# A two-layer graph network on one core: groups of four neighbouring runs of nodes, packed as the mean is transposed

## The chip, the cores and the metric

The kernel runs on one core of one Trainium2 chip. The metric is the device time of one execution in microseconds (us). Before the change the median of three runs is 2605.41 us (2605.15 to 2607.06). The engines are called PE (matmul; PEld its weight load), DVE, ACT, POOL and SP; SP and POOL issue DMAs.

## The reference

The graph has 6250 nodes with rows of 512 floats, and 106250 edges: 50000 random pairs in both directions, and one loop on every node, sorted by `dst`. All is fp32.

```python
# layer 0: mean over the incoming edges, two dense products, residual, layernorm
x_l = x @ W_l.T + b_l
agg = segment_sum(x_l[src], dst);  deg = segment_sum(1, dst)
x = layernorm(x + agg / max(deg, 1) + x @ W_r.T)
# layer 1: mean over the edges by src, relu, residual, layernorm with gamma, beta; then once more
neigh = segment_sum(x[dst] @ W_neigh.T + b_neigh, src) / max(deg, 1)
y = x + relu(x @ W_self.T + b_self + neigh)
x = layernorm(x + layernorm(y) * gamma + beta)
```

The kernel sums the rows of neighbours first and multiplies the mean by the weights afterwards, which is the same by linearity.

## The kernel before, in words

**Tiling.** The sorted edges are cut into chunks of 128, M = 831 in layer 0. Layer 1 needs them by `src`; a sort on the chip, whose steps are spread between the groups of layer 0 (`more(1, True)` and `more(5, False)` in the loop), gives 782 chunks without the loops: every node has one, so layer 1 adds a node's own row instead, and the few loops that occur more than once are found by `loops_beyond_one` and kept apart in `more`.

A **run** is the nodes that begin within 3.5 chunks (`PAIR` = 7 halves; 3 in layer 1, `PAIR_L` = 6), at most H = 32 of them. `place` (L440 on) reads each run's first node from the sorted keys into `lo` (matmul L456) and builds `rel`, the place of each edge's node within its run. If a run had over 32 nodes, or some other condition did not hold, a flag would send the layer to `plain`, a slow loop. There are NW = 238 runs in layer 0, 261 in layer 1. A **group** g is four *distant* runs, c*Q + g for c = 0 to 3, with Q = 60 groups in layer 0 and 66 in layer 1. Run c of the group uses partitions 32c to 32c + 31 in all that follows.

**One group** passes these steps:

- `fetch` (L608): POOL gathers the source rows of each chunk, one indirect DMA of 128 rows for one chunk (L604), into tiles `rows` of four chunks, one of each run. There are `CHUNKS` = 10 buffers; a group takes 3.5 tiles in layer 0 and 3 in layer 1. A tile on the border of two groups is visited by both.
- `match` (L628): one DVE operation compares `rel` with 0 to 31 and gives one-hot matrices `hot`, 128x32 for each chunk and run; `shrink` (L636): ACT copies them to bf16.
- `visits` (L685): PE adds `hot`.T @ rows into `agg` in PSUM, one matmul of 128x32 weights and 512 columns for each chunk and run (L694). The four runs' matmuls lie in four strips of the array side by side; I call the four (eight instructions in fp32) a quad. In layer 1 there is one quad more, with the rows of the repeated loops (`more_rows`).
- `count` (L697): PE sums the one-hots into `deg` (L703); `inverse` (L553): DVE makes `inv` = 1/deg (L557 in layer 1, L560 in layer 0).
- `average` (L708): in layer 1 DVE adds the group's own rows to `agg` (L712); then ACT makes `mean` = agg * inv (L714).
- `turn` and `transposed` (L566): PE transposes `mean` or `own` in four blocks with the identity (L569) into PSUM `tp`, and ACT copies it to SBUF (L571).
- `dense`, `project` (L574): four matmuls of 128x128 weights and 512 columns with each of two weights, into `po` (L577).
- `close`, `finish0`, `finish1`: residual, relu and layernorm on DVE, with ACT for the root (L509).
- `begin` (L669): the group's own rows come in four loads of 32 rows, 64 KB each, on SP (L682); the first row of each is a value in SBUF that SP reads into a register first (L644).
- `store` (L732): four stores of 32 rows from SP, each with such a register (L743). Rows behind a run's last node are overwritten by the run that follows. For three groups (`ends`), POOL stores by indirect DMA instead (L736); in layer 1 these are groups 61, 62 and 65.

**Order.** Instructions run on each engine in the order in which the program names them. The loop (L761 to L790) names for g: fetch and match of g + 1; visits of the first two tiles of g; turn of mean and dense of own of g − 1; store of g − 2; begin of g + 1; visit of the third tile; dense of mean of g − 1; turn of own of g; the other visits, count and average of g; close of g − 1; steps of the sort; shrink of g + 1. So POOL's row of gathers runs ahead as far as there are buffers.

Of the kernel before, what the change touches and what calls it, by code (L numbers as in the profile page):

```python
# [9 lines left out]
F32 = mybir.dt.float32  # L10
# [8 lines left out]
P = 128  # L19
C = 4  # L20
H = P // C
PAIR = 7
PAIR_L = 6
# [75 lines left out]
def kernel(  # L99
# [53 lines left out]
    last, middle = [const.tile([P, P], F32, name=n) for n in ("last", "middle")]  # L153
    for t, row in ((last, P - 1), (middle, P // 2 - 1)):
        nc.vector.tensor_scalar(t, ones, pidx, None, op0=ALU.mult)
        nc.vector.tensor_scalar(t, t, float(row), None, op0=ALU.is_equal)
# [52 lines left out]
    class Sorter:  # L209


        def __init__(self, key, val, layer, pool, ps, loops):
# [4 lines left out]
            pair = self.pair = PAIR_L if loops else PAIR  # L217
            self.half = (pair + 1) // 2
            self.vis = self.half + 1
            self.NW = (2 * self.M + pair - 1) // pair  # L220

            self.Q = (self.NW + 2 * C - 1) // (2 * C) * 2
            Q = self.Q
# [7 lines left out]
            self.X = 1 if loops else 0  # L231
            self.rel = const.tile([P, Q, self.X + self.vis, C], F32, name=f"rel{layer}")
            self.flag = const.tile([1, 1], I32, name=f"flag{layer}")
            if loops:

                a = (E - N - CAP - 1) // P
                self.row = pool.tile([P, M - a], F32, name="row")
                nc.gpsimd.iota(self.row, pattern=[[P, M - a]], base=a * P - (E - N) + LOOP,
                               channel_multiplier=1, allow_small_or_imprecise_dtypes=True)
                self.more = const.tile([P, 1], F32, name="more")  # L240
                self.more_i = const.tile([P, 1], I32, name="more_i")
# [144 lines left out]
        def loops_beyond_one(self):  # L386
# [51 lines left out]
            nc.vector.tensor_scalar(none, self.more, float(N - 1), None, op0=ALU.min)  # L438
            nc.vector.tensor_copy(self.more_i, none)

        def place(self):

            lo, pad, Q, NW = self.lo, self.padded, self.Q, self.NW
            pair, half, vis = self.pair, self.half, self.vis
            mid = middle if pair % 2 else last
            nc.vector.memset(pad[:, 0:1], float(NONE))
            bad = self.fresh()[:1, :2 * NW + C + 2]
            nc.vector.memset(bad, 0.0)
            if self.loops:
                nc.vector.tensor_copy(bad[:, 2 * NW + C:], self.odd)  # L450
            ends = self.ps.tile([P, 2 * D], F32, name="turn")
            ne, no = (NW + 1) // 2, NW // 2

            for a, sel, off, n in ((0, last, 0, ne), (D // 2, mid, half, no),
                                   (D, last, pair - 1, ne - 1), (D + D // 2, last, half - 1, no)):
                nc.tensor.matmul(ends[:, a:a + n], sel, bass.AP(  # L456
                    tensor=pad.tensor, offset=pad.offset + off,
                    ap=[list(pad.ap[0]), [pair, n]]), start=True, stop=True)
            nc.vector.memset(lo, float(N))
            nc.vector.tensor_copy(view(lo, (0, 2, ne, 1)), ends[:, :ne].unsqueeze(2))  # L460
            nc.vector.tensor_copy(view(lo, (1, 2, no, 1)),
                                  ends[:, D // 2:D // 2 + no].unsqueeze(2))
# [4 lines left out]
            nc.vector.tensor_tensor(bad[:, :NW], lo[:1, 1:NW + 1], lo[:1, :NW], op=ALU.subtract)  # L467
            nc.vector.tensor_scalar(bad[:, :NW], bad[:, :NW], float(H), None, op0=ALU.is_gt)
            one = lo[:1, :]
            nc.vector.tensor_tensor(bad[:, NW:NW + ne - 1].unsqueeze(2),  # L470
                                    view(one, (2, 2, ne - 1, 1)),
                                    ends[:1, D:D + ne - 1].unsqueeze(2), op=ALU.is_equal)
            nc.vector.tensor_tensor(bad[:, NW + ne - 1:2 * NW - 1].unsqueeze(2),
                                    view(one, (1, 2, no, 1)),
                                    ends[:1, D + D // 2:D + D // 2 + no].unsqueeze(2),
                                    op=ALU.is_equal)
            for i, (w, e) in enumerate([(Q * c - 2, Q * c) for c in range(1, C)] + [(NW - 3, NW)]):
                t = bad[:, 2 * NW - 1 + i:2 * NW + i]
                nc.vector.tensor_tensor(t, lo[:1, e:e + 1], lo[:1, w:w + 1], op=ALU.subtract)
                nc.vector.tensor_scalar(t, t, float(H), None, op0=ALU.is_lt)  # L480
# [4 lines left out]
            for c in range(C):  # L485
                for i, off in ((0, 0), (1, half)):
                    nodes = bass.AP(tensor=pad.tensor, offset=pad.offset + pair * Q // 2 * c + off,
                                    ap=[list(pad.ap[0]), [pair, Q // 2], [1, vis]])
                    rel = self.rel.rearrange("p (q i) v c -> p q i v c", i=2)[:, :, i, self.X:, c]
                    first = view(lo, (c * Q + i, 2, Q // 2, 1))  # L490
                    nc.vector.tensor_tensor(rel, nodes, first.to_broadcast([P, Q // 2, vis]),
                                            op=ALU.subtract)
            if self.loops:
                nc.vector.tensor_scalar(
                    self.rel[:, :, 0, :], lo[:, :C * Q].rearrange("p (c q) -> p q c", c=C), -1.0,
                    self.more, op0=ALU.mult, op1=ALU.add)
# [56 lines left out]
    def inverse(deg, nr, work, loops=False):  # L553

        inv = work.tile([P, 1], F32, name="inv")
        if loops:
            nc.vector.tensor_scalar(inv[:nr], deg, 1.0, None, op0=ALU.add)  # L557
            nc.vector.reciprocal(inv[:nr], inv[:nr])
            return inv, None
        nc.vector.tensor_scalar(inv[:nr], deg, 1.0, None, op0=ALU.max)  # L560
        nc.vector.reciprocal(inv[:nr], inv[:nr])
        some = work.tile([P, 1], F32, name="some")
        nc.vector.tensor_scalar(some[:nr], deg, 1.0, None, op0=ALU.min)  # L563
        return inv, some

    def transposed(v, nr, name, work, ps):  # L566
        p = ps.tile([P, NK, P], F32, name="tp")
        for k in range(NK):
            nc.tensor.transpose(p[:, k, :nr], v[:nr, k * P:(k + 1) * P], ident[:nr, :nr])  # L569
# [10 lines left out]
    def grouped(s, table, w_n, w_s, layer, finish, dest, other):  # L580


        with tc.tile_pool(name=f"g{layer}", bufs=2) as work, tc.tile_pool(
            name=f"gp{layer}", bufs=1, space=PSUM
        ) as ps:
            M, NW, Q = s.M, s.NW, s.Q
            chunks, hots, state = {}, {}, {}
            ends = Q - 1, (NW - 1) % Q, (NW - 2) % Q
# [6 lines left out]
            def windows(g):  # L595
                return [c for c in range(C) if c * Q + g < NW]

            def own_tiles(g):

                return range(g // 2 * s.pair + (s.half if g % 2 else 0),  # L600
                             g // 2 * s.pair + (s.pair if g % 2 else s.half))

            def gather(t, m):
                nc.gpsimd.indirect_dma_start(  # L604
                    out=t, out_offset=None, in_=table,
                    in_offset=bass.IndirectOffsetOnAxis(ap=s.idx[:, m:m + 1], axis=0))

            def fetch(g):  # L608
                if g == 0 and s.loops:
                    rows = work.tile([P, D], F32, name="more_rows", bufs=1)  # L610
                    nc.gpsimd.indirect_dma_start(
                        out=rows, out_offset=None, in_=table,
                        in_offset=bass.IndirectOffsetOnAxis(ap=s.more_i[:, :1], axis=0))
                    chunks["more"] = {c: rows for c in range(C)}
                for t in ([-1] if g == 0 else []) + list(own_tiles(g)):
                    rows = work.tile([P, C, D], F32, name="rows", bufs=CHUNKS)
                    chunks[t] = {}
                    for c in windows(g):
                        m = c * (Q // 2 * s.pair) + t
                        if 0 <= m < M:  # L620
                            gather(rows[:, c, :], m)
                            chunks[t][c] = rows[:, c, :]

            def visit_tiles(g):
                t = own_tiles(g)
                return ["more"] * s.X + list(range(t.start - 1, t.stop))

            def match(g):  # L628
                hot = work.tile([P, (s.X + s.vis) * C, H], F32, name="hot")
                n = len(visit_tiles(g)) * C  # L630
                both(hot[:, :n], s.rel[:, g].rearrange("p v c -> p (v c)")[:, :n].unsqueeze(2)
                     .to_broadcast([P, n, H]),
                     cols.unsqueeze(1).to_broadcast([P, n, H]), ALU.is_equal)
                hots[g] = hot

            def shrink(g):  # L636
                hb = work.tile([P, (s.X + s.vis) * C, H], BF16, name="hotb", bufs=1)
                n = len(visit_tiles(g)) * C
                nc.scalar.copy(hb[:, :n], hots[g][:, :n])  # L639
                hots[g] = (hots[g], hb)  # L640

            def start(w, t):

                return nc.values_load(  # L644
                    s.lo_i[:1, w:w + 1], engines=[ENG.SP], min_val=0, max_val=t.shape[0] - H,
                    skip_runtime_bounds_check_because="the windows hold: N - H at most, or N "
# [294 lines left out]
```

## Time and profile before

The profile is of one execution, which took 2607.48 us; its span, from the first instruction to the last, is 2605.5 us.

| view | value |
|---|---|
| busy, share of the span | PE 76%, POOL 60%, DVE 40%, ACT 14% |
| granted clock of PE, mean | 0.904 of full speed |
| DMA | mean 192 GB/s, 499.7 MB |
| chain that ended last, by engine | PE 37%, issue 14%, another core or an unknown queue 12%, DVE 9%, SP's queue 4% |
| layer 0, gathers | from 30.4 to 1302 us |
| layer 1, gathers | from 1353.3 to 2559.7 us, the last instruction ends at 2605.5 |
| loads and stores of own rows | 968 DMAs of 64 KB on SP's queue |

How to read it: busy time is what an engine spends in instructions. A line of the groups gives line, engine, operation, output and inputs and count, then the busy time in us and the mean duration in ns, then how long the engine had stood idle just before these instructions and what ended most of that. `<-issue` means that the engine waited for nothing that the profile shows, `<-remote` that nothing on this core is seen to have released it, and `<-PE agg L694` that a matmul of that line did. On the timeline a line is start, duration, engine, operation and count; in brackets stands the idle time ahead of it.

### The profile page before, as it was taken

The numbers are of one execution on the slowest core, as the hardware profiler recorded it, in microseconds if no ns is written. First come the engines' busy times: TensorE is split into PE (matmuls) and PEld (weight loads), VectorE is DVE, ScalarE is ACT, GpSimd is POOL, SyncE is SP. The second block draws the span as 40 slices with busy tenths as digits, with TensorE's granted clock in tenths as the row PEclk, the third lists the DMA queues.
The fourth block names the chain that finished last, engine by engine and source line by source line (L and its number), as shares of the span: only waits on it lengthen the run. The fifth ranks groups of instructions, "written<-read, shape, count | busy, mean of one in ns | idle before, by whom it ended". The sixth has DMA issues, their size and how long they took to land.

```text
span 2605.5 us, 27728 instructions
## 1 busy us (share of the span) xinstructions
PE 1986.7 (76%) x8653; PEld 725.9 (28%) x8653; DVE 1045.7 (40%) x2301; ACT 368.7 (14%) x721; POOL 1554.8 (60%) x1639
## 2 busy tenths in 40 slices
PE   4186876877778676776674888888888888888896
PEld 1022322322322223322220232332323223232332
DVE  2244333344444343211220454444544445454465
ACT  0011111111111111111110111111111111111121
POOL 4566666666666664566526666666656666666641
PEclk9698888888898887898886999999999999999999
DMA  7666766666676664666526676666666676666752
GB/s 222 182 196 203 211 198 204 207 202 202 201 209 202 204 201 147 179 205 205 164 79 183 201 203 202 204 206 204 198 200 204 201 210 199 202 194 204 206 170 59
DMA packets 184614, 499.74 MB, mean 192 GB/s; under 512 B 43962, under 2 KB 46452, under 8 KB 184446
## 3 DMA queue, kind: packets, MB, share of 16 engines
q0 software_dynamic: 130208, 426.37, 56.3%
q1 hardware_dynamic: 51406, 65.89, 8.0%
q10 hardware_dynamic: 2832, 5.51, 0.6%
q8 instruction: 74, 1.21, 0.2%
q14 instruction: 94, 0.77, 0.1%
HBM read 465.01 MB, written 32.96 MB: 191 GB/s over the span
## 4 chain that ended last, share of the span: by engine, by line
PE 37%; issue 14%; another core or an unknown queue 12%; DVE 9%; SPq 4%; ACT 1%; DMA 1%; POOL 0%; DVEq 0%; POOLq 0%; ACTq 0%
PE po L577 19%; PE agg L694 14%; PE tp L569 3%; SPq L743 2%; SPq L644 1%; SPq L682 1%; DVE stats L505 1%; DVE agg L173 1%; DVE po L173 1%; DVE srt L173 1%; ACT mean L714 1%; DVE hot L173 1%; DVE po L515 1%; DVE y L515 1%
## 5 line engine op out<-in xcount | busy, mean ns | idle before, releaser
L604 POOL DMA_INDIRECT rows<-in_x_dram,idx x834 | 799.9, 959 | 468.4 <-issue 238.8
L604 POOL DMA_INDIRECT rows<-h_d,idx x785 | 744.6, 948 | 437.1 <-issue 211.3
L694 PE MATMUL agg<-rows,hot 128*32 128x512 f32 x4220 | 780.1, 633 | 222.9 <-issue 186.0
L577 PE MATMUL po<-wa,meanT 128*128 128x512 f32 (+1 forms) x1008 | 492.2, 633 | 86.8 <-issue 81.3
L577 PE MATMUL po<-wb,ownT 128*128 128x512 f32 (+1 forms) x1008 | 488.6, 630 | 0.3
L694 PEld LDWEIGHTS agg<-rows,hot 128*32 128x32 f32 x4220 | 148.4, 111 | 657.9 <-issue 589.7
L560 DVE TENSOR_SCALAR inv<-deg 128x1 f32<-128x1 f32 (+1 forms) x60 | 9.5, 158 | 786.2 <-remote 312.5
L577 PEld LDWEIGHTS po<-wa,meanT 128*128 128x128 f32 (+1 forms) x1008 | 189.8, 198 | 391.1 <-issue 382.1
L569 PE MATMUL tp<-ident,mean 128*128 128x128 f32 (+1 forms) x504 | 97.5, 325 | 215.0 <-ACT mean L714 146.0
L557 DVE TENSOR_SCALAR inv<-deg 128x1 f32<-128x1 f32 (+1 forms) x66 | 10.5, 158 | 619.6 <-remote 401.4
L577 PEld LDWEIGHTS po<-wb,ownT 128*128 128x128 f32 (+1 forms) x1008 | 196.1, 206 | 207.3 <-issue 204.5
L571 ACT COPY ownT<-tp 128x512 f32<-128x512 f32 (+1 forms) x126 | 73.3, 582 | 1193.2 <-remote 495.9
L173 DVE SCALAR_TENSOR_TENSOR srt<-srt 128x448 f32<-128x448 f32 (+3 forms) x313 | 180.7, 618 | 4.6
L569 PEld LDWEIGHTS tp<-ident,mean 128*128 128x128 f32 (+1 forms) x504 | 63.1, 162 | 350.0 <-ACT mean L714 218.3
L714 ACT ACTIVATE mean<-agg,inv 128x512 f32<-128x512 f32 (+1 forms) x126 | 86.6, 687 | 391.1 <-DVE some L563 83.1
L509 ACT ACTIVATE rstd<-mv,eps 128x1 f32<-128x1 f32 (+1 forms) x192 | 56.6, 295 | 426.1 <-DVE mv L507 204.0
L571 ACT COPY meanT<-tp 128x512 f32<-128x512 f32 (+1 forms) x126 | 72.5, 575 | 183.6 <-remote 122.2
L173 DVE SCALAR_TENSOR_TENSOR hot<-rel,cols 128x640 f32<-128x640 f32 x126 | 96.2, 765 | 0.1
L639 ACT CAST hotb<-hot 128x640 bf16<-128x640 f32 x126 | 86.3, 685 | 24.5 <-DVE hot L173 24.5
L569 PEld LDWEIGHTS tp<-ident,own 128*128 128x128 f32 (+1 forms) x504 | 62.6, 141 | 67.5 <-issue 65.5
L694 PE MATMUL agg<-more_rows,hot 128*32 128x512 f32 x522 | 71.4, 611 | 13.1 <-DMA rows<-h_d,idx 13.1
L569 PE MATMUL tp<-ident,own 128*128 128x128 f32 (+1 forms) x504 | 75.2, 272 | 0.0
(154 smaller groups left out, 968.1 us busy)
## 6 DMA issues: line engine op xcount, KB each, us to landing
own<-h_d SPq DMA_DIRECT2D x261, 64.0 KB
out_dram<-y SPq DMA_DIRECT2D x250, 64.0 KB
own<-in_x_dram SPq DMA_DIRECT2D x230, 64.0 KB
h_d<-y SPq DMA_DIRECT2D x227, 64.0 KB
rows<-in_x_dram,idx POOLq DMA_INDIRECT x834
rows<-h_d,idx POOLq DMA_INDIRECT x785
wa<-in_L_gnn_W_l_dram ACTq DMA_DIRECT2D x1, 1024.0 KB
wb<-in_L_gnn_W_r_dram ACTq DMA_DIRECT2D x1, 1024.0 KB
```

Source lines behind the costliest of these rows:

```text
L173: nc.vector.scalar_tensor_tensor(o, a, 1.0, b, op0=ALU.mult, op1=op)
L505: nc.vector.bn_stats(stats[:nr], v)
L509: nc.scalar.activation(root[:nr], mv[:nr, 1:2], AF.Sqrt, bias=eps[:nr])
L515: nc.vector.tensor_scalar(y, v, mv[:nr, 0:1], root[:nr], op0=ALU.subtract, op1=ALU.mult)
L569: nc.tensor.transpose(p[:, k, :nr], v[:nr, k * P:(k + 1) * P], ident[:nr, :nr])
L571: nc.scalar.copy(t[:, :, :nr], p[:, :, :nr])
L577: nc.tensor.matmul(po[:nr], aT[:, k, :nr], w[:, k, :], start=first and k == 0, stop=end and k == NK - 1)
L604: nc.gpsimd.indirect_dma_start(out=t, out_offset=None, in_=table, in_offset=bass.IndirectOffsetOnAxis(ap=s.idx[:, m:m + 1], axis=0))
L639: nc.scalar.copy(hb[:, :n], hots[g][:, :n])
L694: nc.tensor.matmul(agg[H * c:H * (c + 1), :], hot[:, C * v + c, :], chunks[t][c], start=t == ts[0], stop=t == ts[-1])
L714: nc.scalar.mul(st["mean"][:nr], st["agg"][:nr], st["inv"][:nr])
L743: put.append(nc.sync.dma_start(dest[ds(start(c * Q + g, dest), H), :], y[H * c:H * (c + 1)]))
```

## The change

The runs of a group become *neighbours*. Chunks are dealt in groups of `GROUP` = 14 (layer 0) and `GROUP_L` = 13 (layer 1), a quarter of them to each run (3.5 and 3.25 chunks). There are 60 groups in layer 0 and 61 in layer 1; the last one has 5 and 2 chunks.

- A run's chunks are no longer one in each tile. `tiles` lists them (layer 0: −1 to 3, 3 to 6, 6 to 10, 10 to 13; layer 1: −1 to 3, 2 to 6, 6 to 9, 9 to 12; −1 is the last chunk of the group before), and `order` puts a group's chunks into four tiles by the visit that first needs them: 3, 4, 4 and 3 chunks in layer 0 (3, 6, 10; 0, 4, 7, 11; 1, 5, 8, 12; 2, 9, 13), 3, 4, 4 and 2 in layer 1. In either layer a group makes 18 strip visits, in four full quads and one of two strips. The buffers stay ten.
- The group's nodes lie in consecutive rows, 128 at most. `begin` is one load of 128 rows (256 KB) and `store` one store, with one register each. The store writes 128 rows from the group's first node on; rows behind its last node are overwritten by the group that follows. `agg` still holds run k in partitions 32k on, with gaps. So the mean is packed as it is transposed: `places` (128x128, 0 or 1, one DVE operation) takes the identity's place, in an ordinary fp32 matmul. In layer 0 `some` goes the same way.
- In layer 1 the own row, times one and the number of repeated loops, is added by one matmul of 128x128 weights into `agg`, whose one-hot `match` makes with two more DVE operations. It replaces DVE's addition, the `more` quad and the gather of `more_rows`.
- Only the last two groups of a table without spare rows are loaded (layer 0) or stored (layer 1) by POOL.
- `place` has four selectors and eight matmuls, and gives `place_of` and `back` as well; a new `count_loops` counts the repeated loops of every group in layer 0's time.

In the program, SP's instructions go from 3249 to 1059, PE's program rows from 2611 to 2781, DVE's from 3931 to 4082, ACT's from 1185 to 1155.

```diff
-PAIR = 7
-PAIR_L = 6
+GROUP = 14
+GROUP_L = 13
 CHUNKS = 10
...
+            for k, (t, row) in enumerate(self.before[:C]):
+                f = self.tiles[k][0] - 1
+                g = 1 if f < -1 else 0
+                nc.tensor.matmul(ends[:, k * P:k * P + Q], selectors[:, k * P:(k + 1) * P],
+                                 column(t), start=True, stop=True)
+                nc.tensor.matmul(ends[:, D + k * P + g:D + k * P + Q], last, column(f, g),
+                                 start=True, stop=True)
...
+        def count_loops(self):
...
+            for g in range(0, self.Q, per):
+                n = min(per, self.Q - g)
+                hot = hots[:CAP, :n * P].rearrange("p (g j) -> p g j", j=P)
+                both(hot, rel[:CAP, g:g + n].unsqueeze(2).to_broadcast([CAP, n, P]),
+                     iota[:CAP].unsqueeze(1).to_broadcast([CAP, n, P]), ALU.is_equal)
+                for i in range(n):
+                    nc.tensor.matmul(p[:, g + i:g + i + 1], hot[:, i, :], ones[:CAP, :1],
+                                     start=True, stop=True)
...
-    def transposed(v, nr, name, work, ps):
+    def transposed(v, nr, name, work, ps, places=None):
         for k in range(NK):
-            nc.tensor.transpose(p[:, k, :nr], v[:nr, k * P:(k + 1) * P], ident[:nr, :nr])
+            part = v[:nr, k * P:(k + 1) * P]
+            if places is None:
+                nc.tensor.transpose(p[:, k, :nr], part, ident[:nr, :nr])
+            else:
+                nc.tensor.matmul(p[:, k, :], part, places, start=True, stop=True)
...
             def fetch(g):
-                for t in ([-1] if g == 0 else []) + list(own_tiles(g)):
+                for want in s.order:
                     rows = work.tile([P, C, D], F32, name="rows", bufs=CHUNKS)
...
             def begin(g):
-                for c in windows(g):
-                    nc.sync.dma_start(own[H * c:H * (c + 1)],
-                                      table[ds(start(c * Q + g, table), H), :])
+                    nc.sync.dma_start(own, table[ds(start(g, table), P), :])
...
             def visits(g, some):
+                    if v == s.vis - 1 and s.loops:
+                        nc.tensor.matmul(st["agg"], hot[:, V:].rearrange("p c h -> p (c h)"),
+                                         st["own"], start=False, stop=True)
...
             def average(g):
-                if s.loops:
-                    both(st["agg"][:nr], st["agg"][:nr], st["own"][:nr], ALU.add)
+                st["places"] = work.tile([P, P], F32, name="places", bufs=1)
+                nc.vector.tensor_scalar(st["places"], iota, s.place_of[:, g:g + 1], None,
+                                        op0=ALU.is_equal)
             def turn(g, v):
-                st[v + "T"] = transposed(st[v], st["nr"], v + "T", work, ps)
+                st[v + "T"] = transposed(st[v], P, v + "T", work, ps,
+                                         st["places"] if v == "mean" else None)
...
             def store(g):
-                for c in windows(g):
-                    put.append(nc.sync.dma_start(dest[ds(start(c * Q + g, dest), H), :],
-                                                 y[H * c:H * (c + 1)]))
+                    nc.sync.dma_start(dest[ds(start(g, dest), P), :], y)
...
-                    visits(g, slice(0, 2 + s.X))
+                    visits(g, range(0, 2))
...
-                    visits(g, slice(2 + s.X, 3 + s.X))
+                    visits(g, range(2, 3))
```

## The prediction

> **What bounds the kernel now.** I read the page's costliest groups first, then the table by windows, the waits, and one stretch of the timeline. All durations are of the profiled execution (2607.48 us, span 2605.5 us; 2.1 us above the median of the runs, 2605.41 us).
>
> The groups of the page, busy and idle of the gathers:
>
> ```profile
> L604 POOL DMA_INDIRECT rows<-in_x_dram,idx x834 | 799.9, 959 | 468.4 <-issue 238.8
> L604 POOL DMA_INDIRECT rows<-h_d,idx x785 | 744.6, 948 | 437.1 <-issue 211.3
> ```
>
> Busy and idle together are 1268 and 1182 us: both layers last as long as POOL's row of gathers. The table by windows (us, then busy and count of PE, PEld, DVE, ACT, POOL, the granted clock, DMA share, GB/s):
>
> ```profile
> 600.00:800.00 200.00, 150.22 (x655) 57.25 (x658) 83.02 (x177) 28.95 (x55) 128.36 (x135) 0.89 0.69 203
> 2200.00:2400.00 200.00, 170.97 (x750) 60.98 (x747) 93.57 (x187) 32.56 (x66) 123.93 (x131) 0.96 0.68 201
> ```
>
> PE is busy 75% in layer 0 and 85% in layer 1, POOL 64 and 62%. Neither is full, so they wait for each other. The waits (engine, line, for whom: total us, times, longest):
>
> ```profile
> ACT ownT L571 <- remote: 495.9, 49, 17.3
> POOL rows L604 <- issue: 450.1, 1410, 12.8
> DVE inv L557 <- remote: 401.4, 38, 72.6
> POOL rows L604 <- PE agg L694: 277.1, 81, 23.3
> DVE inv L560 <- remote: 312.5, 19, 70.9
> POOL rows L604 <- remote: 111.6, 49, 8.7
> ```
>
> "Remote" puts 1210 us of ACT's and DVE's waits down to nobody, although what they wait for is a PE result. One cycle of layer 1 on the timeline shows why:
>
> ```profile
> 1741.57 6.74 SPq L743 DMA_DIRECT2D out_dram<-y  x4
> 1742.77 0.60 PE L569 MATMUL tp<-ident,own 128*128 128x128 f32 x4
> 1746.47 0.95 POOL L604 DMA_INDIRECT rows<-h_d,idx  x1 [0.30 <-issue]
> 1749.82 0.59 ACT L571 COPY ownT<-tp 128x512 f32<-128x512 f32 x1 [9.06 <-remote]
> 1750.06 0.16 DVE L557 TENSOR_SCALAR inv<-deg 128x1 f32<-128x1 f32 x1 [8.52 <-remote]
> 1751.05 0.94 POOL L604 DMA_INDIRECT rows<-h_d,idx  x1 [3.64 <-PE agg L694]
> 1752.41 0.88 PE L569 MATMUL tp<-ident,mean 128*128 128x128 f32 x3
> ```
>
> PE ends the turn of own rows at 1743.4; ACT takes it up at 1749.8. The news of PE's work reaches ACT, DVE and POOL only after POOL has run out of row buffers (its last gather ends at 1747.4) and its transfers have drained; then all of it arrives at once. I call this the **freeze**: it begins about a microsecond after SP's first DMA of the cycle. So one cycle is a burst of gathers (1.25 us each: 0.95 busy, 0.30 issue), a gap of some 2.4 to 3.3 us beyond the usual 0.30, and one pass of the chain deg, inv, mean, its turn. From one turn of a mean to the next, 20.6 us pass on average in layer 0 and 18.05 in layer 1.
>
> **The change, part by part.**
>
> *Gathers and cycles.* Layer 0: 834 gathers become 831, layer 1: 786 with the repeated loops become 782; −4 and −5 us. Of layer 0's 1268 us, 834 x 1.25 = 1042 are gathers; 226 us are gaps: five long ones (8.7, 7.9, 23.3, 9.8, 13.5 = 63 us, from the sorting between groups) and 163 us in some 61 common ones, 2.7 each. With four tiles a group and the first tile's buffers held to the last visit, one burst is a group of 14 gathers: (831 − 35)/14 = 57 gaps, 57 x 2.75 = 157. That is −6. Layer 1: 1182 − 785 x 1.25 = 200 us in some 61 gaps, 3.3 each; after, (782 − 36)/13 = 57 gaps, 57 x 3.25 = 185: −15.
>
> *PE, per group.* In: a true fp32 matmul with a 0/1 matrix for the turn of the mean. An fp32 matmul is two instructions here (L577: 1008 instructions for 126 groups, eight for four blocks). L569 takes 0.49 to 0.66 us for its four, 0.12 to 0.16 each; eight at that rate make 1.0 to 1.3 us, +0.6. L456, an fp32 matmul of 131 columns, takes 2.23 us for eight: +1.6. L577's rate (eight of 512 columns in 3.60 us) cut to 128 gives 0.9, +0.4. I take +1.0, between the two nearest, and keep +0.4 and +1.6. Layer 0 besides: a half quad of strips costs a whole one (L694's quads of three strips take as long as those of four, 1.0 us), +0.5 on average, and `some` through the matrix, 2 x 0.11: **+1.7** in all. Layer 1: that half quad in place of the `more` quad (1.0 for 0.89) and one 128x128x512 matmul for own, 0.9 (two instructions of L577, eight of which pass in 3.60 us): **+2.0**. By the windows PE is busy 0.751 x 20.6 = 15.5 us a group in layer 0 and 0.855 x 18.05 = 15.4 in layer 1; after, 17.2 and 17.4. The new cycles are 14 x 1.25 + 2.75 = 20.25 and 13 x 1.25 + 3.25 = 19.5 us, so PE is covered, with 3.05 and 2.1 us to spare; what it costs if not, the first rival tells. Layer 1's deg, inv, mean chain is shorter by DVE's agg + own (0.70 us, between inv and mean).
>
> The Trainium skill ("TensorE: Matmul & The Clock Gate", Terms, xbus) states that TensorE's transpose mode is 4 times faster for fp32, which speaks against the packing matmul. By it the turn would take 4 x 0.49 to 0.66, 2.0 to 2.6 us, an estimate, and this step +1.5 to +2.0 in place of +1.0.
>
> *DVE and ACT.* Per group the places matrix (128x128 is_equal, about 0.23 to 0.30 by the rows of 128x128 tensor_scalar), in layer 1 two more for own's one-hot, less the 0.70. DVE is 42 to 47% busy; it costs nothing unless it comes between inv and mean, and there places stands behind inv, beside ACT's mean (0.69 us).
>
> *SP.* Eight register loads and eight DMAs of 64 KB a group become two and two of 256 KB, the same bytes. A store now covers 128 rows and the next group's overlaps it, so stores wait for each other; they are a group apart. What this does to the freeze no row shows. If two DMAs start it as eight do: 0. If it vanishes, POOL runs without gaps, at most −(157 + 185) = −342 us (less the 2 us that one cycle needs at a switch). The burst at the start speaks for 0: PE's chain stood still (inv waited 70.85 us, to 103.58) while POOL gathered to 99.4, though SP had issued nothing since 42. I take 0. In a sentence apart: the Trainium skill ("DMA: Bandwidth & Descriptors", Issuing engines are not separate DMA queues) says that all queues interleave on the same 16 engines and another issuer saves issue time only; by that rule, too, the sum would be 0, whereas the remote waits show that more than bytes is at stake.
>
> *Sorting, once.* place() has four selectors and eight matmuls, and count_loops is nine rounds of a DVE op (1.09 us, the row of 128x896) and seven fp32 matmuls of one column (14 instructions at 0.11, L430's 28 in 3.15 us): 9 x 2.6 = 24 us on PE and DVE in layer 0, in one stretch, as before the 23.3 us gap came from such a stretch. POOL's lookahead may hide it (0); fully visible with place 30. I take +20, and +3 for layer 0's own place ahead of the first gather.
>
> *Ends.* Layer 1's stores of two end groups stood in POOL's queue among the gathers: one held POOL 22.73 us for y (2523.7 to 2547.4) and 1.3 for itself, then came nine gathers and the end. After, POOL's stores belong to the last two groups, behind all gathers: −24. Both layers' final drain passes two groups: +4 each.
>
> **Sum:** layer 0: −4 −6 +20 +3 +4 = +17. Layer 1: −5 −15 −24 +4 = −40. Together −23: 2607.5 − 23 = 2584.5, as an unprofiled run 2.1 less, about 2582. I say **2583**.
>
> **The rivals.**
>
> *Slower: PE becomes the late one.* A freeze costs PE too: it idles 20.6 − 15.5 = 5.1 us a group in layer 0 and 2.6 in layer 1. If those waits stay whole, the added 1.7 and 2.0 make 22.3 and 20.05 us against POOL's cycles of 20.25 and 19.5: 57 x 2.05 + 57 x 0.55 = +148, that is 2731. It decides once more than 3.05 us (layer 0) or 2.1 us (layer 1) of wait stay. For it: ten buffers are now 2.5 groups instead of 2.9 and 3.3, and the third tile of a group waits for the last visit two groups back, so POOL hangs on PE's end, not its middle. Against it: most of PE's wait stands where POOL's drain does, so a longer burst gives it room.
>
> *Faster: the freeze goes with the small DMAs.* POOL without gaps: 17.5 and 16.25 us a group; PE's 17.4 then binds layer 1: 57 x 2.75 + 57 x 2.1 = −277, about 2306. For it: each freeze begins behind an SP DMA. Against it: the start, above.
>
> *Shorter freeze.* One DMA starts later or is drained sooner; half of that gain, −60 to −180: about 2460.
>
> *The change doesn't do what it says:* runs of over 32 nodes would send a layer to the plain loop, far above 3000 us. A run holds 448 or 416 edges of nodes with 17 or 16 on average, 26 nodes; not likely.
>
> **Chances.** Forecast case 0.42 (2540 to 2630), PE late 0.31 (2630 to 2760), shorter freeze 0.12, no freeze 0.14, fallback 0.01. Bounds of the unknown costs (+0.4 to +1.6 us of matmul, 0 to 30 of sorting, −342 of the freeze) lie within these cases. The range 2400 to 2760 leaves out no freeze and a little of both neighbours. About 0.2% (5.2 us) is what a measurement here tells from no change: faster 0.27 + 0.12 + 0.14 = 0.53, same 0.05, slower 0.11 + 0.31 = 0.42. The first case alone would be 2540 to 2630.
>
> **What would show it.** Right: bursts of 14 and 13 gathers with one gap of 2.5 to 3.5 us, remote waits of ACT and DVE still near 1000 us, PE 85 to 89% busy in both layers, no POOL store among layer 1's gathers, some 20 us without gathers near 1050. Wrong: POOL's gaps at 5 us or more with "PE agg" as releaser (PE late), or gathers without gaps (no freeze); the turn of the mean at under 0.9 us or over 2.2 would mis-size PE's step.

## The result, and the profile after

The changed kernel takes 2668.85 us (median of four runs, 2663.95 to 2674.65) against 2606.23 us before: ratio 1.024, 95% interval 1.0217 to 1.0263. The forecast was 2583 us. The time lies in the stated range, but on the other side of no change. The profiled execution has a span of 2664.8 us, 59.3 us more than before.

The gathers' groups on the page, and the changed kernel's waits:

```profile
L645 POOL DMA_INDIRECT rows<-in_x_dram,idx x831 | 801.2, 964 | 532.5 <-issue 219.1
L645 POOL DMA_INDIRECT rows<-h_d,idx x782 | 745.7, 954 | 491.9 <-issue 207.6
```

```profile
DVE inv L596 <- PE deg L729: 564.2, 79, 14.0
ACT meanT L614 <- remote: 547.0, 76, 14.3
...
POOL rows L645 <- PE agg L716: 221.1, 60, 54.9
POOL rows L645 <- remote: 182.1, 80, 7.1
...
DVE inv L596 <- remote: 175.5, 8, 56.3
ACT ownT L614 <- remote: 158.6, 13, 17.2
```

Busy and idle of the gathers sum to 1334 and 1238 us (1268 and 1182 before): with fewer gathers, POOL stands longer in both layers. The silence that the prediction calls the freeze is still there (I call it the standstill as well), but it has moved: before, ACT's `ownT` and DVE's `inv` were what waited most for a "remote" releaser, now it is `meanT`, which PE needs at once for the product with the mean. So PE's own waits have moved in front of that product (before, then after):

```profile
L577 PE MATMUL po<-wa,meanT 128*128 128x512 f32 (+1 forms) x1008 | 492.2, 633 | 86.8 <-issue 81.3
L620 PE MATMUL po<-wa,meanT 128*128 128x512 f32 x968 | 543.9, 714 | 378.4 <-issue 217.8
```

In layer 1, PE stands over 5 us there in 28 of the 61 groups, in this trace and in a second one of the same kernel (e5 below), and in none in the two traces of the kernel before. The windows of layers 0 and 1 (columns as before):

```profile
600.00:800.00 200.00, 158.84 (x704) 64.39 (x700) 84.21 (x189) 27.88 (x52) 128.65 (x134) 0.88 0.68 199
...
2200.00:2400.00 200.00, 155.21 (x706) 61.61 (x705) 81.22 (x182) 29.79 (x58) 124.16 (x131) 0.88 0.68 198
```

PE is busy 79 and 78%; in layer 1 it fell from 85%, though it has more to do, and its granted clock fell from 0.96 to 0.88. One pair of groups of layer 1, on the timelines of POOL (only the gathers that end a gap), PE and ACT:

```profile
2009.88 0.94 POOL L645 DMA_INDIRECT rows<-h_d,idx  x1 [3.09 <-remote]
...
2018.52 0.95 POOL L645 DMA_INDIRECT rows<-h_d,idx  x1 [3.94 <-PE agg L716]
...
2031.80 0.95 POOL L645 DMA_INDIRECT rows<-h_d,idx  x1 [2.20 <-PE tp L610]
...
2050.84 0.94 POOL L645 DMA_INDIRECT rows<-h_d,idx  x1 [3.01 <-remote]
```

```profile
2010.02 5.96 PE L620 MATMUL po<-wa,meanT 128*128 128x512 f32 x8 [9.71 <-ACT meanT L614]
2015.81 0.60 PE L610 MATMUL tp<-ident,own 128*128 128x128 f32 x4
2016.34 1.91 PE L716 MATMUL agg<-rows,hot 128*32 128x512 f32 x12
2018.18 1.13 PE L722 MATMUL agg<-own,hot 128*128 128x512 f32 x2
...
2021.22 1.16 PE L612 MATMUL tp<-places,mean 128*128 128x128 f32 x8
...
2026.74 3.70 PE L620 MATMUL po<-wa,meanT 128*128 128x512 f32 x8
...
2035.69 1.16 PE L612 MATMUL tp<-places,mean 128*128 128x128 f32 x8
```

```profile
2009.38 0.59 ACT L614 COPY meanT<-tp 128x512 f32<-128x512 f32 x1 [12.47 <-remote]
...
2048.24 0.59 ACT L614 COPY meanT<-tp 128x512 f32<-128x512 f32 x1 [10.41 <-remote]
```

Two groups take 40.96 us (2009.88 to 2050.84) and have three gaps: bursts of 4, 9 and 13 gathers. In the first, silence catches PE between the turn of the mean and its product; PE stands 9.71 us, and after the news has come it needs 8.2 us to its last visit, while POOL has only four gathers to do: the third gap. The other group passes without being held, in 14.5 us from turn to turn. Part of the 8.2 us is PE's clock: from 2010 to 2013 us, after the stand, it was granted 0.50, and the product took 5.96 us where the other group's took 3.70. By my estimate from these two rows, 2.3 of the 3.6 us by which the third gap exceeds 0.30 come with that.

The prediction let the freeze begin about a microsecond after SP's first DMA. Here it does not: SP issues at 2028.81, the news of `deg` still passes at once (PE ends at 2033.90, DVE begins at 2033.94), and only the turn's, at 2036.85, is held, until 2048.24.

Where the 59.3 us come from, read from the timelines: a gap is what a gather stands beyond the usual 0.30 us, a long one is over 6 us. The column "2nd pair" is a second pair of traces (e5 and e6 below). The last one is a pair without the standstill, of two sets: e13 is the kernel before, and e12 stands for the changed kernel, with its transfers cut in four again; the changed kernel itself was not run without the standstill.

| term, us | forecast | measured | 2nd pair | no standstill |
|---|---|---|---|---|
| first gather later | +3 | +2.0 | +1.5 | +1.9 |
| layer 0, long gaps (sorting) | +20 | +25.8 | +33.8 | +42.7 |
| layer 0, common gaps | −6 | +29.2 | +5.9 | −1.2 |
| layer 0, gathers themselves | −4 | +0.3 | −1.5 | −1.9 |
| last gather of layer 0 to first of layer 1 | +4 | −6.6 | −4.7 | +9.7 |
| layer 1, long gaps (POOL's store) | −24 | −25.3 | −26.4 | 0 |
| layer 1, common gaps | −15 | +20.3 | +22.6 | −1.3 |
| layer 1, gathers themselves | −5 | −1.1 | −0.7 | −5.4 |
| last gather to the end | +4 | +14.6 | +15.1 | +9.5 |
| sum | −23 | +59.3 | +45.7 | +54.0 |

### The profile page after: what moved, and what is told of

Its sections match the earlier page's. It is cut to its first block, busy times and chain, and to the rows that moved or that the text cites. A ratio compares the mean times of both kernels' runs of the same rounds, so it can differ in the third digit from the quotient of the medians.

```text
span 2664.8 us, 25479 instructions
## 1 busy us (share of the span) xinstructions
PE 2011.1 (75%) x9073; PEld 825.0 (31%) x9073; DVE 1038.3 (39%) x2434; ACT 366.9 (14%) x691; POOL 1552.3 (58%) x1628
## 3 DMA queue, kind: packets, MB, share of 16 engines
q8 instruction: 76, 1.25, 0.2%
## 5 line engine op out<-in xcount | busy, mean ns | idle before, releaser
L620 PE MATMUL po<-wa,meanT 128*128 128x512 f32 x968 | 543.9, 714 | 378.4 <-issue 217.8
L716 PE MATMUL agg<-rows,hot 128*32 128x512 f32 x4352 | 704.4, 621 | 78.3 <-issue 56.4
L596 DVE TENSOR_SCALAR inv<-deg 128x1 f32<-128x1 f32 x121 | 19.2, 159 | 1131.3 <-PE deg L729 564.2
L620 PE MATMUL po<-wb,ownT 128*128 128x512 f32 x968 | 445.8, 603 | 0.0
L620 PEld LDWEIGHTS po<-wa,meanT 128*128 128x128 f32 x968 | 210.9, 229 | 715.9 <-issue 538.7
L620 PEld LDWEIGHTS po<-wb,ownT 128*128 128x128 f32 x968 | 177.4, 194 | 176.7 <-issue 176.7
L612 PE MATMUL tp<-places,mean 128*128 128x128 f32 x968 | 148.5, 299 | 94.6 <-ACT mean L736 51.4
L612 PEld LDWEIGHTS tp<-places,mean 128*128 128x128 f32 x968 | 124.6, 201 | 206.7 <-ACT mean L736 110.4
L736 ACT ACTIVATE mean<-agg,inv 128x512 f32<-128x512 f32 x121 | 83.2, 687 | 335.0 <-DVE inv L597 202.9
L666 ACT CAST hotb<-hot 128x768 bf16<-128x768 f32 (+1 forms) x121 | 92.5, 764 | 32.5 <-issue 26.5
L610 PE MATMUL tp<-ident,own 128*128 128x128 f32 x484 | 72.7, 273 | 0.0
```

The costliest lines, as they stand in the source:

```text
L610: nc.tensor.transpose(p[:, k, :nr], part, ident[:nr, :nr])
L612: nc.tensor.matmul(p[:, k, :], part, places, start=True, stop=True)
L620: nc.tensor.matmul(po[:nr], aT[:, k, :nr], w[:, k, :], start=first and k == 0, stop=end and k == NK - 1)
L666: nc.scalar.copy(hb, hots[g])
L716: nc.tensor.matmul(st["agg"][H * k:H * (k + 1), :], hot[:, C * v + k, :], chunks[m], start=k not in st["begun"], stop=v == len(ts) - 1 and ...
L736: nc.scalar.mul(st["mean"], st["agg"], st["inv"])
```

## The experiments

The sets ran on several chips, and the kernel before took 2569.07 and 2568.41 us in two of them and 2135 to 2137 us in four. In those four no standstill is in any trace: gathers follow each other every 1.25 us without gaps, and the list of waits has no remote one. Each kernel is compared with the kernel before in its own set. Theories: **A**, PE's added work makes PE the late one (the prediction's slower rival); **B**, POOL lacks buffers ahead; **F**, SP's DMAs set off the silence; **G**, how news is held sets the cycle, and PE's length does not; **S**, the sorting is most of the loss.

**The changed kernel (e5) and the one before (e6), again, with the standstill.**

> The changed kernel itself, run beside the kernel before on the chip of this set. The kernel of the first set ran on a chip on which PE's news came without a standstill (gathers without gaps, 1.25 us each). Theory S (the sorting steps are most of the loss): where gathers run without gaps, the changed kernel takes 40 to 60 us more than before, of which the gap near the count is some 35, and its ratio is near 1.025; where there are gaps, 1.02 to 1.03 as well. Rival (the loss is in the gaps of each group): without gaps the ratio is within 1.01 of one.

> The kernel before itself, for a trace on the same chip as the other kernels of this set. With gathers without gaps: layer 0 about 834 x 1.25 = 1043 us plus the gap of the sorting (10 to 15 us), layer 1 786 x 1.25 = 983 us, span near 2135. With the standstill: as in the trace of before, 2605.

Measured: 2621.38 us, ratio 1.0209 (1.0184 to 1.0233); the set has the standstill. The table's "2nd pair" is this one.

**The count of loops (S; e1).** One matmul in place of 61, and of nine one-hots:

```diff
-            for g in range(0, self.Q, per):
...
-                for i in range(n):
-                    nc.tensor.matmul(p[:, g + i:g + i + 1], hot[:, i, :], ones[:CAP, :1],
-                                     start=True, stop=True)
+            nc.vector.tensor_scalar(a, first, self.more[:CAP], None, op0=ALU.is_le)
+            nc.vector.tensor_scalar(b, nxt, self.more[:CAP], None, op0=ALU.is_gt)
+            both(b, a, b, ALU.mult)
+            both(a, first, b, ALU.mult)
...
+            nc.vector.tensor_scalar(place, iota[:CAP], j, None, op0=ALU.is_equal)
+            nc.tensor.matmul(p[:, :Q], place, b, start=True, stop=True)
```

> The changed kernel with the repeated loops of all groups counted by one matmul (64 rows, a one-hot of the place against a one-hot of the group) in place of nine one-hots on DVE and 61 matmuls of one column. In the changed kernel's trace these 61 matmuls and their one-hots take PE from 1084 to 1124 us, and POOL stands 54.9 us without a gather there. Theory 1 (the count stands in the path of the gathers): about 38 us less than the changed kernel, 2625 to 2635, and the gap near 1126 us shrinks to under 20 us. Rival (the stretch is filled by buffers, and the gap moves elsewhere): under 10 us less.

Measured, without the standstill: 2156.67 us, ratio 1.0093 (1.0076 to 1.011). Two kernels of the same set that keep the old count are at 1.0236 and 1.0262. The gap at the count is 9.8 us in place of 43.5 and 44.5. So S holds where there is no standstill: some 30 to 35 of the 50 to 55 us. What the old count does in the changed kernel, on PE's and POOL's timelines:

```profile
1088.52 3.12 PE L534 MATMUL turn<-ones,srt 64*128 64x1 f32 x14 [13.02 <-DVE srt L172]
1092.81 3.15 PE L534 MATMUL turn<-ones,srt 64*128 64x1 f32 x14 [1.18 <-DVE srt L172]
...
1118.73 5.49 PE L534 MATMUL turn<-ones,srt 64*128 64x1 f32 x24 [1.18 <-DVE srt L172]
1124.16 3.38 PE L716 MATMUL agg<-rows,hot 128*32 128x512 f32 x16
```

```profile
1126.35 0.95 POOL L645 DMA_INDIRECT rows<-in_x_dram,idx  x1 [54.87 <-PE agg L716]
```

Fourteen instructions take 3.15 us, 0.22 each, and DVE and PE take turns; the visits that would free buffers stand behind them, from 1072 to 1124 us.

**PE's added work (A against G; e2, e9, e14).** The edits, in e2 the first one alone:

```diff
-                                         st["places"] if v == "mean" else None)
+                                         None)
...
-                    if v == s.vis - 1 and s.loops:
-                        nc.tensor.matmul(st["agg"], hot[:, V:].rearrange("p c h -> p (c h)"),
-                                         st["own"], start=False, stop=True)
```

> The changed kernel with the mean turned by the identity (a transpose, four instructions) in place of the packing matmul (eight), everything else kept; the rows are not packed, so the mean's rows stand at the wrong nodes. Theory A (PE's added work a group is the loss): the turn falls from 1.16 to about 0.55 us, 121 groups, so 50 to 75 us less than the changed kernel, near 2600. Theory B (the buffers that the gathers wait for decide, and PE's turn lies in time in which PE waits anyway): under 25 us less.

> The changed kernel without PE's added work in a group: the mean is turned by the identity (a transpose) and the matmul that adds the own rows in layer 1 is left out, so the rows are not packed and own rows are missing from the sums. PE's group falls from 14.5 to about 12.9 us in layer 1 and by 0.6 us in layer 0. Theory A (PE's added work is the loss of each group): on a chip with the standstill 60 to 140 us less than the changed kernel (ratio to before 0.97 to 1.0). Theory G (what sets the cycle is how PE's news is held while POOL gathers, not PE's length): within 25 us of the changed kernel, ratio 1.01 to 1.03. On a chip without it: ratio 1.02 to 1.025, as the turn alone changed nothing there.

> The changed kernel without packing matmul (turned by the identity; rows not packed) and without the own matmul (own rows left out of the sums), on another chip. With the standstill: theory A (PE's added work is the loss of each group) 60 to 140 us less than the changed kernel, ratio to before 0.97 to 1.0; theory G (the held news sets the cycle, not PE's length) ratio 1.01 to 1.03. Without it: 1.02 to 1.025, as before.

Measured, all without the standstill: 2186.4 us (1.0236), 2186.39 us (1.0229) and 2182.55 us (1.0228), beside 2191 us for the kernels with the full work and split transfers (e4, e12). There PE's work costs next to nothing: layer 1's 782 gathers take 978 to 982 us, 1.25 each, with or without it. For the case with the standstill these say nothing.

**SP's DMAs (F; e4, e12).** Four loads and four stores of 32 rows in place of one and one:

```diff
-                    nc.sync.dma_start(own, table[ds(start(g, table), P), :])
+                    for c in range(C):
+                        nc.sync.dma_start(own[H * c:H * (c + 1)],
+                                          table[ds(start(g, table) + H * c, H), :])
...
```

> The changed kernel with the one load and the one store of a group cut into four of 32 rows, each with its register, as before the change: eight DMAs of 64 KB a group in place of two of 256 KB, everything else kept. Theory F (SP's DMAs set off the standstill of PE's news): the remote waits grow and the time by 30 us or more. Rival (the standstill hangs on POOL's gathers alone; SP's issues are hidden): within 13 us of the changed kernel, 2656 to 2682.

> The changed kernel with the one load and the one store of a group cut into four of 32 rows each, as in the first set, whose chip showed no standstill. Theory F (SP's DMAs set it off): with the standstill, 30 us or more above the changed kernel, ratio to before 1.035 or more. Rival (it hangs on the gathers alone): within 13 us, ratio 1.015 to 1.03.

Measured: 2191.65 us (1.0262) and 2190.89 us (1.0256), both without the standstill. From its first gather to the end, layer 1 takes 1023.0 and 1021.5 us here, and 1024.3 us in e1, whose layer 1 is the changed kernel's: the joined transfers, the change's plainest saving, are worth nothing that can be told there. What they do to a standstill was not measured.

**Buffers (B).** A buffer for each chunk, 40 of them, alone (e7) and with the cheap count (e8); and eight tiles in place of ten (`CHUNKS = 8`; e10, e15). Twelve tiles (e3) gave no time: they need 127.25 KB a partition, and 111.69 were left.

```diff
-                    rows = work.tile([P, C, D], F32, name="rows", bufs=CHUNKS)
...
+                            rows = work.tile([P, D], F32, name="rows", bufs=C * CHUNKS)
```

> The changed kernel with a buffer for each chunk (40 buffers of one chunk) in place of ten tiles of four: 2.9 and 3.1 groups ahead in place of 2.5, since no place of a tile stays empty, and no chunk is held by the other chunks of its tile. Theory B (buffers held too long make the extra gaps): with the standstill, the gaps fall to one a group, 40 to 70 us less than the changed kernel; without it, some 10 us less, since more lies ahead when the sorting holds PE. Theory A (PE is late whatever lies ahead): within 10 us of the changed kernel either way.

> The changed kernel with both edits: the repeated loops counted by one matmul, and 40 buffers of one chunk. If the losses are the count and the held buffers, and these add up: with the standstill 75 to 110 us less than the changed kernel, that is below the kernel before by 0.5 to 2%; without it 40 to 55 us less, within 0.7% of the kernel before. If the count alone matters: 33 to 40 us less either way.

> The changed kernel with eight tiles of rows in place of ten, two groups ahead in place of 2.5. With the standstill: theory G (PE's news comes when POOL stands, so that more lookahead only makes longer silences, as 40 single buffers made the kernel slower) says the same or up to 40 us less than the changed kernel; theory B (POOL's lookahead is what is missing) says 40 us more or worse. Without the standstill: 10 to 60 us more than the changed kernel, since POOL then hangs on PE's last visit with a PE that is busy 96%.

> The changed kernel with eight tiles of rows, on another chip. With the standstill: theory G (news comes when POOL stands) the same as the changed kernel or up to 40 us less, ratio 1.005 to 1.025; theory B (lookahead is missing) 40 us more, ratio 1.035 or above. Without it: 1.028 as measured.

Measured with the standstill: e7 2666.19 us, 1.0366 (1.0329 to 1.0402), e8 2638.05 us, 1.0276. B falls: more groups ahead and finer release made the kernel 45 us slower than the changed kernel of the same set, with more and smaller gaps (113 in layer 1 in place of 83). A's number, within 10 us, did not come either, and why it is slower was not found. The cheap count takes 28 us off e7 as well; but e8, of which at least 33 us less than the changed kernel were expected, is 17 us slower than it. Without the standstill eight tiles give 2196.71 and 2199.07 us (1.0281 and 1.0302): some 6 to 8 us above e12, the gap at the count being 50 to 52 in place of 43 us. What eight tiles do in the standstill stays open.

**Round trips pulled apart (e11, e16, with the cheap count), and the kernel before without the standstill (e13).** The order of the loop:

```diff
+                    visits(g, range(s.vis))
+                    count(g)
+                    average(g)
+                if 0 < g <= Q:
                     turn(g - 1, "mean")
...
+                    dense(g - 2, "own")
...
+                    dense(g - 2, "mean")
...
+                    turn(g - 1, "own")
...
+                    close(g - 2)
```

> The changed kernel with the cheap count and with PE's round trips pulled apart: all visits of a group stand together, the mean is turned one group later, and its product is made another group later, so that each thing that PE sends to another engine and needs back has some 7 to 13 us on the way; nine tiles of rows, four own tiles. Theory G (PE loses by waiting, in the standstill, for the answers of ACT and DVE): PE no longer stands there, the cycle is POOL's burst and one gap, and the time falls to 0.90 to 0.97 of the kernel before with the standstill. Rival (POOL's waits for buffers set the cycle whatever PE does): 1.00 to 1.03. Without the standstill: 1.0 to 1.02.

> The changed kernel with the cheap count and PE's round trips pulled apart, on another chip. With the standstill: theory G (PE loses by standing for answers) ratio 0.90 to 0.97; rival (POOL's waits for buffers set the cycle whatever PE does) 1.00 to 1.03. Without it: 1.03 as measured.

> The kernel before, for its trace on the chip of this set. If its gathers run without gaps: layer 0 about 1045 us from first to last gather with at most 12 us of gaps, layer 1 985 us, the last gather 45 us before the end, and then the loss of the changed kernel without a standstill (some 50 us) is the count (34) and the longer place and turn at layer 0's start and ends (16). If it has the standstill: as the trace of before.

Measured: 2203.67 us (1.0311) and 2207.72 us (1.0343), without the standstill: above the 1.0 to 1.02 expected, and 47 us more than e1, for nothing gained. The trace of before (e13) gives the table's last column: 42.7 of 54 us are the sorting's gap, and the two drains (19.2 us), less what gathers and common gaps gave back, make up the rest; the common gaps are gone from both kernels.

**Layer by layer.** Two kernels with one of the edits above in each layer, in e17

```diff
-                    rows = work.tile([P, C, D], F32, name="rows", bufs=CHUNKS)
+                    rows = work.tile([P, C, D], F32, name="rows", bufs=CHUNKS if layer else 8)
```

and PE's two edits in layer 1, in e18 the loop of e11 in layer 0 and the same two in layer 1:

> The changed kernel with one edit in each layer, to be read layer by layer from the trace. Layer 0: eight tiles of rows in place of ten. Layer 1: the mean turned by the identity and no own matmul (rows not packed, own rows left out of the sums), PE's group 1.6 us shorter. Layer 0 lasts to the first gather of layer 1, layer 1 from there to the end. With the standstill the kernel before has shares of 0.519 and 0.481 of its span in them, the changed kernel 1.026 and 1.008 times these. Theory A (PE's added work makes the gaps of layer 1): layer 1 at 0.94 to 0.98 of before's. Theory G (not PE's length): 0.99 to 1.02. Layer 0: theory G 1.01 to 1.03, theory B (lookahead missing) 1.05 or more. Without the standstill neither edit matters.

Measured: 2197.57 us, 1.0288, again without the standstill; it repeats what e9 and e10 showed (gap at the count 52 us, layer 1 without gaps).

> The changed kernel with one edit in each layer. Layer 0: PE's round trips pulled apart (all visits together, the mean turned one group later, its product another group later; nine tiles). Layer 1: the mean turned by the identity and no own matmul (rows not packed, own rows left out of the sums). With the standstill, against before's layers (0.519 and 0.481 of its span): theory A (PE's added work makes the gaps) puts layer 1 at 0.94 to 0.98, theory G (held news, not PE's length) at 0.99 to 1.02 and layer 0 at 0.90 to 0.98; if buffers decide whatever PE does, layer 0 at 1.00 to 1.04. Without the standstill: layer 0 1.03 to 1.05 of before's (the count and its place), layer 1 1.00.

Measured, with the standstill: 2561.07 us, 0.9971 (0.9955 to 0.9988). Layer 1, with the light PE, lasts 1187.5 us; the kernel before has 1234.9 in e6, the changed one 1245.5 in e5: 0.962 of before's, as A said, and 58 us less than the changed kernel. These are other sets, but the kernel before took 2568.41 us in one and 2569.07 us in the other. The gathers of layer 1 that end a gap, in this kernel:

```profile
1858.14 0.94 POOL L645 DMA_INDIRECT rows<-h_d,idx  x1 [2.80 <-remote]
...
1876.98 0.94 POOL L645 DMA_INDIRECT rows<-h_d,idx  x1 [2.91 <-remote]
...
1895.77 0.94 POOL L645 DMA_INDIRECT rows<-h_d,idx  x1 [2.83 <-remote]
```

One burst of 13, one gap, 18.8 us a group: the cycle that the prediction had drawn for the changed kernel. In the same stretch (1450 to 2450 us) its waits read

```profile
ACT ownT L614 <- remote: 409.3, 41, 10.1
DVE inv L596 <- remote: 408.2, 43, 10.7
PEld agg L716 <- issue: 321.2, 435, 2.7
```

The silence is as long as ever, but it falls on `ownT` and `inv`, with PE's visits beside it, as in the kernel before; `meanT` is not in it, and no group of layer 1 has PE standing before the product with the mean (28 have in e5). G falls for layer 1. Which of the two edits does it was not told apart. Layer 0, pulled apart, lasts 1371.0 us (1366.2 in e5): its common gaps fell from 71 to 52 and from 157 to 127 us, and the sorting's long gaps rose from 81 to 107, the switch to layer 1 from 44.9 to 49.6. That is 1.03 of the kernel before's 1331.1 us (e6), the number of G's rival and not G's; but the common gaps did fall, and what they gave was lost at the sorting, so the number does not settle it.

**Larger groups (e19).** With the cheap count and

```diff
-GROUP = 14
-GROUP_L = 13
+GROUP = 15
+GROUP_L = 14
```

> The changed kernel with the cheap count of loops and larger groups, 15 chunks in layer 0 and 14 in layer 1: 56 groups in each layer in place of 60 and 61, so nine groups' PE work (some 14.5 us each) less, and bursts of 18.8 and 17.5 us in place of 17.5 and 16.3. Theory A (PE's work against the length of a burst makes the third gap in two groups): with the standstill one gap a group, 112 in place of 150, and 80 to 130 us less than the changed kernel, ratio to before 0.97 to 0.99. Theory G or B: 40 to 60 us less, ratio 1.0 to 1.01. Without the standstill the gathers set the pace: 33 to 50 us less, ratio 1.0 to 1.01.

Measured, with the standstill: 2544.74 us, 0.9902 (0.9871 to 0.9932): faster than both kernels, by some 24 us than before. Against its own set it is A's ratio, at the edge; the 112 gaps that A expected did not come. It has 138 common gaps (154 in e5, 111 in e18) and nine groups fewer for PE. The cheap count alone is some 30 of the 77 us between it and e5; layer 1, which the count does not touch, lasts 1208.0 us in place of 1245.5. Without the standstill it was not run.

## Why the prediction was wrong

- **"PE is covered, with 3.05 and 2.1 us to spare"** is the step that failed. It set PE's busy time against POOL's cycle, as if PE could work in the whole of it. In the standstill it cannot: from turn to turn of layer 1 (1500 to 2550 us) 20.1 us pass, PE is busy in 15.7 and idle in 4.4, where the sum had 2.1 to spare and the kernel before has 2.6 idle. What counts is whether the news of the turn of the mean gets out before it stops, so that its product can follow. With 1.6 us less work (e18) it does, and layer 1 keeps one gap a group; with the added work the silence falls between turn and product in nearly one group of two, and a third gap comes to the pair. Layer 1's common gaps are +20.3 us where −15 was forecast. From e18 to e5 it is 58 us, 0.95 for each of 61 groups, for an added work whose size I had about right: the turn takes 1.16 us where four transposes take 0.49 to 0.66 (+0.5 to +0.7, forecast +1.0), and the own matmul ends within 1.13 (forecast 0.9).
- **The factor for transposes.** The Trainium skill, "TensorE: Matmul & The Clock Gate" (Terms, xbus), states a factor of 4 for fp32 in transpose mode; here the matmul takes 1.16 us against 0.49 to 0.66, a factor of 1.8 to 2.4, and the measurement decides.
- **57 gaps a layer.** There are 78 and 87, of 2.4 us each, where 2.75 and 3.25 were forecast. The forecast also began too low: counted in the same way the kernel before has 70 and 67 common gaps, not 61 and 61. In layer 0 part of it is chance: the same kernel has 71 in e5, where the common gaps cost 5.9 us, not 29.2. Why two executions of two sets differ so was not found, and layer 0's common gaps stay unexplained.
- **The sorting, +20**, was +26 to +43: the term was mis-sized. I priced the 122 instructions by L430 (0.11 us, weights of 64 columns); with 128 columns they took 0.22. The cheap count took back 28 us with the standstill and 30 to 35 without it.
- **The ends, +4 −24 +4 = −16**, gave −17 (−6.6 −25.3 +14.6): right in sum, not in its parts. Perhaps PE had caught up while POOL's early store stood there, which no run shows; without it the last drain is 10 us longer than I said. Where there is no standstill, the store had not held any gather, and both drains cost 19 us.
- **SP's transfers, 0**: right without the standstill (e4, e12 against e1, layer 1), not tested with it. The rival "the freeze goes" came true in other sets, but not by the change: the kernel before is without it there, too.
- Right were the remote waits near 1000 us (ACT's and DVE's three rows above are 994 with `some_there`'s 112.9) and the missing POOL store; wrong were the size of a common gap (2.4 us, not 2.5 to 3.5) and PE's share (79 and 78%, not 85 to 89).

The slower rival had the direction, that PE's waits do not give way to its added work, and its range (2630 to 2760) held the time; I gave it 0.31. Its sum was luck in part: it has 20.05 us a group for layer 1, and 20.1 came, but as 15.7 busy and 4.4 idle, not as 17.4 and 2.6. Its sign, gaps of 5 us or more released by `agg`, did not come outside the sorting: there are more gaps, not longer ones.

## What to carry to other kernels

A step that runs once, in the queue of an engine that frees buffers, was paid nearly in full here: count its instructions with the row of the same weight shape, and ask what is queued behind it. Slack is not cycle minus busy time where an engine's answers are held up: look which of its round trips falls into the hold, and what the added microsecond moves into it. Fewer groups, each as full as its partitions allow, were, together with the cheap count, the one edit that beat both kernels while computing all of the sums (e19, 2544.74 us); ask for it where every group has a fixed price on the engine that runs late.

## What was not expected of the hardware

- The same program differs by 20 to 22% from set to set: 2135 us without the standstill, 2568 to 2606 with it. Without it the trace has no remote wait at all, the clock granted to PE was 0.98 (e13) in place of 0.90 (before), and layer 1's windows show PE busy 98%. What brings the standstill was not found: the records give one chip number to a set of either kind (e9 to e12 without, e18 and e19 with), so that it need not belong to a chip; it comes on behind SP's DMAs in the timelines, but not at a fixed distance (above), and no run took these away while it was there.
- More buffers ahead with finer release made a kernel slower (e7, 45 us). That PE's news passes only when POOL stands would explain it, but no run shows that this is the reason.
